# Layer 2 of a two-layer network: other places for the gate projections, the copies of the sums and the gates in a hand-written schedule

## The chip, the cores and the metric

The kernel runs on one core of one Trainium2 chip. The metric is the device time of one launch in microseconds, as the median of several runs. A profile of one further run gives each instruction's start and duration.

## The reference, cut to what matters

The program has two residual layers on an image of shape (4, 192, 128, 128). The first layer (Fourier transforms and convolutions) isn't touched by the change. The second is a selective state-space layer, with 128 x 128 = 16384 tokens per image:

```python
seq = (seq - mu) * lax.rsqrt(var + LN_EPS) * ln_g + ln_b
xz = jnp.einsum('blc,ec->ble', seq, in_proj_w)
xs, z = jnp.split(xz, 2, axis=-1)
...
u = jax.nn.silu(xc).transpose(0, 2, 1)
x_dbl = jnp.einsum('bld,kd->blk', u, x_proj_w)
dt, Bm, Cm = jnp.split(x_dbl, [DT_RANK, DT_RANK + D_STATE], axis=-1)
dt = jax.nn.softplus(jnp.einsum('blr,dr->bld', dt, dt_proj_w) + dt_proj_b)
A = -jnp.exp(A_log)
def step(hcar, inp):
    dt_t, B_t, C_t, u_t = inp
    dA = jnp.exp(dt_t[..., None] * A)
    hnew = hcar * dA + (dt_t * u_t)[..., None] * B_t[:, None, :]
    y_t = jnp.sum(hnew * C_t[:, None, :], axis=-1)
    return (hnew, y_t)
...
y = ys.transpose(1, 0, 2) + u * Dp
y = y * jax.nn.silu(z)
out = jnp.einsum('bld,cd->blc', y, out_proj_w)
```

There are 384 inner channels and 16 states. xc is a causal convolution of xs with four taps, and x comes in normalised by groups of channels. The scan over tokens is the heart of it: a decay dA, an input (dt times u times B), and a sum over states of h times C.

## The kernel before

The tokens are cut into chunks of T = 512, 32 per image, 128 in all. The 384 inner channels are three tiles of 128 partitions (j = 0, 1, 2). The 16 states are taken two at a time, so a chunk has 3 x 8 = 24 groups, k = 0 to 23; sg = k mod 8 counts within a tile. All four images run through one long list of groups (`order`), and the order of every instruction on every engine is written out by hand: nothing is scheduled automatically (`tc.manual_schedule()`).

What a group needs on the engines:

- **ACT** (ScalarE) makes the decays `da`, exp(dt A), in `decay` (L788). For most groups `early` writes them to on-chip memory four states ahead. For the groups whose inputs POOL makes (`BY_POOL`: sg 1, 4, 7, in the last tile 1 and 7), `decay_there` writes them to a PSUM buffer (`op` in the profile) three scans ahead, after the scan that frees it.
- **DVE** (VectorE) runs two scans (L856), one for each state, and for most groups the inputs' products (L808). For groups in `BY_POOL`, **POOL** (GpSimd) makes the inputs `db` (L816). For the group sg = 6 (`BY_PE`), PE turns dtu (`turned`, L822), ACT scales the four blocks for each of two states (`scaled`, L831, eight operations), and PE turns them back (`turned_back`, L842). `skip` (L896) then scales u by Dp. `TURNED` says in which group this is done for each tile.
- **POOL** multiplies h by C (`hc`, L869), and makes dtu (L745).
- **PE** (TensorE) adds the two states' hc into `py`, turned, three groups later (`sums`, L882; `LAG` = 3). There is one such PSUM buffer. After a tile's eight groups ACT copies it out (`evacuate`, L891), PE turns it back (`turn`, L911), and DVE multiplies it by silu(z) (`gate`, L916). The next tile's first sums wait for the copy. `add_skip` (L901) adds the scaled u right after those first sums, in the group sg = 3.

`front(i)` makes a chunk's inputs: the normalised x (L606), the mean's matmuls (L614) and the subtraction (L616), squares (L621), variance (L629), root (L635), reciprocal (L637), its turn (L640), copy (L643) and spread (L647), the scaling (L651), the in-projections (L657), the convolution as four matmuls a tile in two halves (L675), silu for u and z (L683, L687), the x projection (L724), its copy (L727), the store of B and C for the broadcast loads (L729, L762), the dt projections (L737), softplus (L741), and the transposes for bT (L751, L754). It is a generator that goes on by one `yield` per group. It starts at k = 14 of a chunk, for the chunk two ahead. A plain yield goes on before the group's scans; `yield MID` goes on after the group's first scan, `yield LATE` after the second. `finish` (the output projection, L925, adding to x, L931, and the store, L934) runs the same way from group 6 of the next chunk. Projections, turns and convolutions share three PSUM buffers (`psum()`).

The loop over groups around the change:

```python
                def between():
                    if done:
                        evacuate(*before)
                    go_on(parts[MID])
                    if pos >= NG and sg == LAG + 2:
                        gate(*before)

                scans(pos, n, k, between)
                go_on(parts[LATE])
```

`between` is called after the first of the group's two scans.

Of the kernel before, what the change touches and what calls it, by code (L numbers as in the profile page):

```python
# [10 lines left out]
F32 = mybir.dt.float32  # L11
# [16 lines left out]
NJ = DI // 128  # L28
NS = 16
RANK = 12  # L30
T = 512
# [472 lines left out]
def layer1(tc, xmid, out, st2, w, n_tok=S * S):  # L504
# [7 lines left out]

    BY_POOL = ((1, 4, 7), (1, 4, 7), (1, 7))
    BY_PE = 6
    TURNED = {1: 0, 10: 1, 16: 2}
    MID, LATE = "mid", "late"
    with ExitStack() as ctx:
        def pool(name, bufs, **kw):
# [64 lines left out]
        def psum():  # L583
            return ps1.tile([128, 512], F32, name="ps")
# [14 lines left out]
        def front(i):  # L599

            b, ch = divmod(i, NCHUNK)
            g = got[i]
            xm = g["xm"]
            s = lp.tile([CH, 2, T], F32, name="s", bufs=2)
            for t in range(2):
                nc.scalar.activation(  # L606
                    s[:, t, :], xm[:, t, :], AF.Identity,
                    bias=nmr[:, b, t : t + 1], scale=st2[:, b, t, 1:2],
                )
            yield  # L610
            yield
            mu = psum()
            for t in range(2):
                nc.tensor.matmul(mu[0:CH], ones[0:CH, :], s[:, t, :], start=t == 0, stop=t == 1)  # L614
            yield LATE
            nc.vector.scalar_tensor_tensor(  # L616
                s, _bc(mu[0:CH], 1, 2), -1.0 / C, s, ALU.mult, ALU.add
            )
            yield
            sq = lp.tile([128, NJ, T + 3], F32, name="xs")[0:CH, 0:2, 0:T]  # L620
            nc.scalar.activation(sq, s, AF.Square)  # L621
            yield
            yield


            var = psum()
            for q in range(4):
                for t in range(2):
                    nc.tensor.matmul(  # L629
                        var[:, q : q + 1], sq[:, t, q * 128 : (q + 1) * 128], ones[0:CH, 0:1],  # L630
                        start=t == 0, stop=t == 1,
                    )
            yield
            rs = tp.tile([128, 4], F32, name="rs")
            nc.scalar.activation(rs, var[:, 0:4], AF.Sqrt, bias=eps, scale=1.0 / C)  # L635
            yield LATE
            nc.vector.reciprocal(rs, rs)  # L637
            yield
            rt = psum()
            nc.tensor.transpose(rt[0:4, 0:128], rs, ident)  # L640
            yield MID
            rows = tp.tile([4, 128], F32, name="rows")
            nc.scalar.copy(rows, rt[0:4, 0:128])  # L643
            yield
            rb = psum()
            for q in range(4):
                nc.tensor.matmul(  # L647
                    rb[0:CH, q * 128 : (q + 1) * 128], sel[:, q, :], rows, start=True, stop=True
                )
            yield LATE  # L650
            nc.vector.tensor_tensor(s, s, _bc(rb[0:CH], 1, 2), ALU.mult)  # L651
            yield

            def in_proj(m):
                pp = psum()
                for t in range(2):
                    nc.tensor.matmul(  # L657
                        pp, wiT[:, t, m * 128 : (m + 1) * 128], s[:, t, :], start=t == 0, stop=t == 1
                    )
                return pp  # L660

            xs = lp.tile([128, NJ, T + 3], F32, name="xs")
            if ch == 0:
                nc.gpsimd.memset(xs[:, :, 0:3], 0.0)
            else:
                nc.scalar.copy(xs[:, :, 0:3], halo)
            for j in range(NJ):
                pp = in_proj(j)
                yield
                nc.scalar.activation(xs[:, j, 3:], pp, AF.Identity, bias=bxz[:, j : j + 1])  # L670
            nc.scalar.copy(halo, xs[:, :, T : T + 3])

            def conv(j, pc, half):
                for k in (2 * half, 2 * half + 1):
                    nc.tensor.matmul(  # L675
                        pc, dcw[:, j, k, :], xs[:, j, k : k + T], start=k == 0, stop=k == 3
                    )

            u, zs = g["u"], g["zs"] = {}, {}

            def silu_u(j, pc):
                u[j] = jp.tile([128, T], F32, name="u")
                nc.scalar.activation(u[j], pc, AF.Silu, bias=cb[:, j : j + 1])  # L683

            def silu_z(j, pp):
                zs[j] = jp.tile([128, T], F32, name="zs", bufs=5)
                nc.scalar.activation(zs[j], pp, AF.Silu, bias=bxz[:, NJ + j : NJ + j + 1])  # L687

            c0 = psum()
            conv(0, c0, 0)  # L690
            yield
            conv(0, c0, 1)
            yield
            c1 = psum()
            conv(1, c1, 0)
            yield
            yield
            yield
            conv(1, c1, 1)
            yield  # L700
            yield
            silu_u(0, c0)
            silu_u(1, c1)
            yield LATE
            c2 = psum()
            conv(2, c2, 0)
            yield
            conv(2, c2, 1)
            yield
            z0 = in_proj(NJ)  # L710
            yield
            yield
            silu_u(2, c2)
            silu_z(0, z0)
            yield LATE
            z1 = in_proj(NJ + 1)
            yield
            z2 = in_proj(NJ + 2)
            yield
            silu_z(1, z1)  # L720
            silu_z(2, z2)
            px = psum()
            for j in range(NJ):
                nc.tensor.matmul(px, xpT[:, j, :], u[j], start=j == 0, stop=j == NJ - 1)  # L724
            yield
            xd = tp.tile([128, T], F32, name="xd", bufs=1)
            nc.scalar.copy(xd, px)  # L727
            dbc = g["dbc"] = dram.tile([2, NS, T], F32, name="dbc")
            nc.sync.dma_start(out=dbc.rearrange("a s t -> (a s) t"), in_=xd[96:, :])  # L729
            yield  # L730
            dt, dtu = g["dt"], g["dtu"] = {}, {}


            d = [psum() for _ in range(NJ)]
            for j in range(NJ):
                rows = slice(32 * j, 32 * j + RANK)
                nc.tensor.matmul(d[j], dtT[rows, :], xd[rows, :], start=True, stop=True)  # L737
            yield
            for j in range(NJ):
                dt[j] = jp.tile([128, T], F32, name="dt")  # L740
                nc.scalar.activation(dt[j], d[j], AF.Softplus, bias=dtb[:, j : j + 1])  # L741
            yield
            for j in range(NJ):
                dtu[j] = jp.tile([128, T], F32, name="dtu")
                nc.gpsimd.tensor_tensor(dtu[j], dt[j], u[j], ALU.mult)  # L745
            yield

            bt = psum()
            for blk in range(T // 128):
                at = slice(blk * 128, (blk + 1) * 128)  # L750
                nc.tensor.transpose(bt[:, at], xd[:, at], ident)  # L751
            yield LATE
            g["bT"] = tp.tile([128, T // 128, G], F32, name="bT")
            nc.scalar.copy(  # L754
                g["bT"],
                bt.rearrange("p (k c) -> p k c", c=128)[:, :, 96 + BY_PE * G : 96 + (BY_PE + 1) * G],
            )

        def load_bc(i, sg):

# [157 lines left out]
        def finish(n):  # L918
# [3 lines left out]
            for t in range(2):  # L922
# [6 lines left out]
                yield  # L929
                yield MID  # L930
                nc.vector.tensor_add(xm[:, t, :], po[0:CH], xm[:, t, :])  # L931
                if t == 0:
                    yield
            nc.sync.dma_start(  # L934
                out=out[b][:, ch * T : (ch + 1) * T].rearrange("(t p) f -> p t f", p=CH), in_=xm
            )
# [18 lines left out]
        def go_on(fs):  # L955
            for f in fs:
                next(f, None)

        with tc.manual_schedule():
# [21 lines left out]
            for pos, (n, k) in enumerate(order):  # L981
# [1 line left out]
                if k == FRONT:  # L983
                    start_front(n + 2)
                if k == NGR - 2 and n + 1 < total:
                    assert len(fronts) == (n + 2 < total), fronts
                parts = {MID: [], LATE: []}
                step(tails, parts)

                done = pos >= NG and sg == LAG  # L990
                before = n - (j == 0), (j - 1) % NJ
                if sg == BY_PE - 1:
                    turned_back(G * (pos + 1))
                if pos >= LAG and sg != LAG:
# [10 lines left out]
                    inputs(*order[pos + 2])  # L1005

                def between():
                    if done:
                        evacuate(*before)
                    go_on(parts[MID])  # L1010
                    if pos >= NG and sg == LAG + 2:
                        gate(*before)

                scans(pos, n, k, between)
                go_on(parts[LATE])
                if k in TURNED:
                    scaled(n, TURNED[k], 0)
# [2 lines left out]
                if pos >= LAG and sg == LAG:  # L1020
                    sums(*order[pos - LAG])
                    add_skip(n, j)
                if k == LAG + 2 and n:
                    tails.append(finish(n - 1))
                if k == LAG + 7 and n + 2 < total:
                    load_x(n + 2)
                if k >= NGR - BCL and n + 1 < total:
                    load_bc(n + 1, k - (NGR - BCL))
# [148 lines left out]
```

## Time and profile before

| | |
|---|---|
| median of 3 runs | 12280.62 us (12278.13 to 12304.0) |
| profiled execution | 12415.77 us, span 12414.0 us |
| DVE busy | 10827.1 us, 87% of the span |
| PE busy | 10437.2 us, 84% |
| POOL busy | 10088.6 us, 81% |
| ACT busy | 9075.5 us, 73% |
| mean granted TensorE clock | 0.871 |

The busy shares are over both layers. The first layer takes the first eighth of the span, and DVE and POOL are less busy there. In the second layer each chunk repeats the same instructions, so windows of one chunk (some 85 us) and the timeline within it tell more than the shares. In the timelines a row has the start, the time, the engine, line and operation, and in brackets how long the engine sat idle before it and on whom it waited. Neighbouring DVE operations overlap a little, so starts are further guides than durations.

### The profile page before, as it was taken

The page shows a single profiled execution, that of the slowest core. Times are in us where ns is not written, and L with a number is a line of the kernel's source. Part 1 is how long each engine was busy: PE and PEld are TensorE (multiplying, and loading weights), DVE is VectorE, ACT ScalarE, POOL GpSimd, SP SyncE. Part 2 cuts the span into 40 slices and gives each one's busy share as a digit, 9 for nine tenths or more (in the row PEclk, how much of TensorE's full clock was granted, in tenths as well). Part 3 has the DMA queues.
Part 4 walks back from the last instruction along what each step waited for, and adds up shares of the span by engine and source line. Part 5 has one row for each costly group of instructions (what it writes and reads, how often), then busy time and mean ns, then how long its engine had stood idle before and what let it go on. Part 6 is the DMA issues. An engine that isn't in the chain of part 4 may idle for free.

```text
span 12414.0 us, 146878 instructions
## 1 busy us (share of the span) xinstructions
PE 10437.2 (84%) x49034; PEld 7035.5 (57%) x49034; DVE 10827.1 (87%) x11581; ACT 9075.5 (73%) x17891; POOL 10088.6 (81%) x4598
## 2 busy tenths in 40 slices
PE   4778888888888888888888888888888888888887
PEld 2434465555555656555555555565555555555565
DVE  5565499999999999999999899999999999999998
ACT  2322287787887877877878878778888878878777
POOL 0000199999999999999999899999999999999998
PEclk8878688888888888888888888888999888998888
DMA  8787533333323323323333233233233233233232
GB/s 212 208 215 193 165 108 102 117 106 107 117 101 112 117 94 116 113 99 117 106 107 117 99 113 117 95 115 114 98 119 119 99 113 118 99 113 117 97 114 90
DMA packets 503760, 1490.32 MB, mean 120 GB/s; under 512 B 67889, under 2 KB 118774, under 8 KB 502486
## 3 DMA queue, kind: packets, MB, share of 16 engines
q1 hardware_dynamic: 482518, 1418.00, 35.6%
q0 software_dynamic: 13312, 50.34, 1.2%
q10 hardware_dynamic: 7168, 12.59, 0.3%
q8 instruction: 385, 6.31, 0.2%
q14 instruction: 377, 3.09, 0.1%
HBM read 1325.19 MB, written 155.32 MB: 119 GB/s over the span
## 4 chain that ended last, share of the span: by engine, by line
ACT 34%; DVE 28%; PE 18%; issue 15%; POOL 3%; DMA 2%; SPq 0%; DVEq 0%; POOLq 0%; ACTq 0%
DVE h L856 18%; PE py L882 7%; ACT da L788 6%; DVE op L808 6%; ACT dbT L831 6%; ACT L788 5%; ACT op L788 4%; PE ps L675 2%; POOL hc L869 2%; PE py L901 2%; ACT u L896 2%; PE pr L471 2%; ACT dt L741 1%; ACT s L606 1%; ACT zs L687 1%
## 5 line engine op out<-in xcount | busy, mean ns | idle before, releaser
L869 POOL TENSOR_TENSOR hc<-h,bc 128x1024 f32<-128x1024 f32 x3072 | 7196.1, 2362 | 900.9 <-DVE h L856 874.8
L856 DVE TENSOR_TENSOR_SCAN h<-da,carry,op 128x512 f32<-128x512 f32 x3968 | 4896.7, 1262 | 0.3 <-DVE rs L637 0.3
L882 PE MATMUL py<-ident,hc 128*128 128x128 f32 x24576 | 3709.6, 303 | 987.1 <-ACT yt L891 574.4
L882 PEld LDWEIGHTS py<-ident,hc 128*128 128x128 f32 x24576 | 3252.7, 158 | 2085.9 <-issue 1876.2
L788 ACT ACTIVATE da<-dt,c_A_log 128x512 f32<-128x512 f32 x4096 | 2788.1, 715 | 89.6 <-DVE h L856 83.1
L856 DVE TENSOR_TENSOR_SCAN h<-op,carry,db 128x512 f32<-128x512 f32 x1984 | 2513.3, 1267 | 137.8 <-ACT op L788 135.8
L816 POOL TENSOR_TENSOR db<-dtu,bc 128x1024 f32<-128x1024 f32 x1024 | 2417.9, 2361 | 5.7 <-DMA bc<-dbc 5.7
L788 ACT ACTIVATE op<-dt,c_A_log 128x512 f32<-128x512 f32 x2048 | 1404.0, 686 | 1310.0 <-DVE h L856 1308.4
L808 DVE TENSOR_TENSOR op<-dp,bc 128x512 f32<-128x512 f32 x3328 | 2229.1, 670 | 35.9 <-DMA bc<-dbc 35.9
L675 PE MATMUL ps<-xs,dcw 128*128 128x512 f32 x3072 | 1486.2, 613 | 206.1 <-ACT u L683 206.1
L657 PE MATMUL ps<-s,c_wiT 96*128 96x512 f32 x3072 | 1465.1, 599 | 84.0 <-DVE s L651 84.0
L788 ACT ACT_TABLE_LOAD x636 | 816.0, 1283 | 214.4 <-DVE h L856 205.3
L675 PEld LDWEIGHTS ps<-xs,dcw 128*128 128x128 f32 x3072 | 562.4, 201 | 698.4 <-issue 462.0
L657 PEld LDWEIGHTS ps<-s,c_wiT 96*128 96x128 f32 x3072 | 533.9, 190 | 551.6 <-issue 407.3
L831 ACT ACTIVATE dbT<-ps,bT 128x128 f32<-128x128 f32 x3072 | 831.4, 376 | 0.0
L867 ACT COPY carry<-h 128x2 f32<-128x2 f32 x3072 | 550.1, 185 | 380.3 <-DVE h L856 374.9
L916 DVE TENSOR_TENSOR yg<-ps,zs 128x512 f32<-128x512 f32 x384 | 265.2, 691 | 534.4 <-PE ps L911 534.4
L925 PE MATMUL ps<-yg,c_woT 128*96 128x512 f32 x1536 | 700.7, 592 | 0.0
L477 POOL DMA_DIRECT2D xmid<-xt x64 | 42.6, 666 | 786.4 <-DVE xt L475 780.2
L737 PE MATMUL ps<-xd,c_dtT 12*128 12x512 f32 x768 | 457.0, 786 | 264.6 <-ACT dbT L831 263.3
L745 POOL TENSOR_TENSOR dtu<-dt,u 128x512 f32<-128x512 f32 x384 | 477.4, 1271 | 33.5 <-ACT dt L741 33.5
L842 PE MATMUL op<-ident,dbT 128*128 128x128 f32 x3072 | 463.9, 274 | 1.2 <-DVE h L856 1.2
(173 smaller groups left out, 11187.2 us busy)
## 6 DMA issues: line engine op xcount, KB each, us to landing
bc<-dbc SPq DMA_DIRECT2D x1024, 1024.0 KB, 5.4
xt<-in_x SPq DMA_DIRECT2D x192, 768.0 KB, 8.9
xmid<-xt POOLq DMA_DIRECT2D x64, 768.0 KB, 7.1
xm<-xmid SPq DMA_DIRECT2D x128, 384.0 KB, 3.5
out<-xm SPq DMA_DIRECT2D x128, 384.0 KB, 3.0
d<-x ACTq DMA_DIRECT2D x64, 192.0 KB, 6.9
df<-u SPq DMA_DIRECT2D x16, 512.0 KB, 5.0
u<-df SPq DMA_DIRECT2D x16, 512.0 KB, 12.3
```

What stands on the lines that cost most here:

```text
L657: nc.tensor.matmul(pp, wiT[:, t, m * 128 : (m + 1) * 128], s[:, t, :], start=t == 0, stop=t == 1)
L675: nc.tensor.matmul(pc, dcw[:, j, k, :], xs[:, j, k : k + T], start=k == 0, stop=k == 3)
L745: nc.gpsimd.tensor_tensor(dtu[j], dt[j], u[j], ALU.mult)
L788: nc.scalar.activation(da, got[n]["dt"][j], AF.Exp, scale=A[:, j, st : st + 1])
L808: nc.vector.tensor_tensor(dbs[s], g["dp"], g["bc", k % NG][:, 0, q, :], ALU.mult)
L816: nc.gpsimd.tensor_tensor(db, _bc(g["dtu"][j], 1, G), g["bc", sg][:, 0], ALU.mult)
L831: nc.scalar.activation(t[:, blk, :], g["tu", j][:, blk, :], AF.Identity, scale=g["bT"][:, blk, q : q + 1])
L856: nc.vector.tensor_tensor_scan(h[:, q, :], das.pop(s), dbs.pop(s) if db is None else db[:, q, :], 0.0 if ch == 0 else g["before"][:, j, st ...
L867: nc.scalar.copy(g["carry"][:, j, sg * G : (sg + 1) * G], h[:, :, T - 1])
L869: nc.gpsimd.tensor_tensor(hc, h, g["bc", sg][:, 1], ALU.mult)
L882: nc.tensor.matmul(py[:, blk, :], hc[:, q, blk * 128 : (blk + 1) * 128], ident, start=first, stop=sg == NG - 1 and q == G - 1 and blk == T ...
L925: nc.tensor.matmul(po[0:CH], woT[:, j, t * CH : (t + 1) * CH], g["yg", j], start=j == 0, stop=j == NJ - 1,)
```

## The change

In the changed kernel:

- `TURNED` is {2: 0, 10: 1, 14: 2} where it was {1: 0, 10: 1, 16: 2}.
- The copy of the sums comes after the second scan of the group sg = 2, ahead of `scaled`; it came after the first scan of sg = 3.
- The gate comes before the first scan of the group sg = 6; it came after the first scan of sg = 5.
- In `front`, the mean's matmuls come a group sooner, and the subtraction after the first scan of its group instead of the second. The root and the reciprocal come a group sooner; the scaling by the root comes in the group after, between its scans. The in-projections of xs, their copies and the first convolution come a group later.
- The first z projection comes two groups later and its silu one. The second and third z projections go from groups 13 and 14 to groups 21 and 23, and their silu from group 15 to group 0 of the next chunk. zs has four buffers, not five. So the front of one chunk is still running when two others' work begins, and the assertion counts one more.
- The dt projections are issued after the second scan of group 17 instead of before the first, and softplus after the first scan of group 18.
- The additions to x, the output's store and the next load of x come a group later.

```diff
-    TURNED = {1: 0, 10: 1, 16: 2}
+    TURNED = {2: 0, 10: 1, 14: 2}
...
             yield
-            yield
             mu = psum()
...
-            yield LATE
+            yield
+            yield MID
             nc.vector.scalar_tensor_tensor(
...
             nc.scalar.activation(sq, s, AF.Square)
             yield
-            yield
+            yield LATE
             var = psum()
...
             yield
+            yield MID
             rs = tp.tile([128, 4], F32, name="rs")
...
             yield
+            yield LATE
             rb = psum()
...
-            yield LATE
+            yield
+            yield MID
             nc.vector.tensor_tensor(s, s, _bc(rb[0:CH], 1, 2), ALU.mult)
...
-                zs[j] = jp.tile([128, T], F32, name="zs", bufs=5)
+                zs[j] = jp.tile([128, T], F32, name="zs")
...
             conv(1, c1, 0)
             yield
             yield
-            yield
             conv(1, c1, 1)
...
             conv(2, c2, 0)
             yield
+            yield
             conv(2, c2, 1)
             yield
+            yield
             z0 = in_proj(NJ)
             yield
-            yield
             silu_u(2, c2)
             silu_z(0, z0)
-            yield LATE
-            z1 = in_proj(NJ + 1)
-            yield
-            z2 = in_proj(NJ + 2)
-            yield
-            silu_z(1, z1)
-            silu_z(2, z2)
+            yield
             px = psum()
...
             nc.sync.dma_start(out=dbc.rearrange("a s t -> (a s) t"), in_=xd[96:, :])
             yield
+            yield LATE
             dt, dtu = g["dt"], g["dtu"] = {}, {}
...
                 nc.tensor.matmul(d[j], dtT[rows, :], xd[rows, :], start=True, stop=True)
             yield
+            yield MID
...
                 bt.rearrange("p (k c) -> p k c", c=128)[:, :, 96 + BY_PE * G : 96 + (BY_PE + 1) * G],
             )
+            yield
+            z1 = in_proj(NJ + 1)
+            yield
+            yield
+            z2 = in_proj(NJ + 2)
+            yield
+            silu_z(1, z1)
+            silu_z(2, z2)
...
                 nc.vector.tensor_add(xm[:, t, :], po[0:CH], xm[:, t, :])
-                if t == 0:
-                    yield
+                yield
...
-                done = pos >= NG and sg == LAG
                 before = n - (j == 0), (j - 1) % NJ
+                if pos >= NG and sg == LAG + 3:
+                    gate(*before)
...
                 def between():
-                    if done:
-                        evacuate(*before)
                     go_on(parts[MID])
-                    if pos >= NG and sg == LAG + 2:
-                        gate(*before)
 
                 scans(pos, n, k, between)
+                if pos >= NG and sg == LAG - 1:
+                    evacuate(*before)
                 go_on(parts[LATE])
...
-                if k == LAG + 2 and n:
+                if k == LAG + 3 and n:
                     tails.append(finish(n - 1))
-                if k == LAG + 7 and n + 2 < total:
+                if k == LAG + 8 and n + 2 < total:
                     load_x(n + 2)
```

More of the change, by code (lines that the diff above doesn't have):

```diff
@@ L985, in layer1 @@
                 if k == NGR - 2 and n + 1 < total:
-                    assert len(fronts) == (n + 2 < total), fronts
+                    assert len(fronts) == 1 + (n + 2 < total), fronts
                 parts = {MID: [], LATE: []}
                 step(tails, parts)
-                done = pos >= NG and sg == LAG
                 before = n - (j == 0), (j - 1) % NJ
+                if pos >= NG and sg == LAG + 3:
+                    gate(*before)
                 if sg == BY_PE - 1:
```

## The prediction

> **What bounds the kernel now.** I read the time by slices first: from 1.5 ms on every slice looks alike, so the second layer is 128 equal chunks, and one chunk is worth reading closely. Successive starts of the reciprocal (L637) in the trace are mostly 85.33 us apart, with stretches at 83.4 to 83.8; the mean of 126 steps is 84.97. A window of one chunk gives the engines' shares:
>
> ```profile
> core 0: us, PE busy (x) PEld busy (x) DVE busy (x) ACT busy (x) POOL busy (x), PEclk, DMA share, GB/s
> 5018.69:5104.02 85.33, 73.23 (x358) 50.61 (x357) 78.00 (x83) 68.14 (x137) 78.05 (x36) 0.88 0.31 108
> ```
>
> DVE and POOL each have 78 us of work and idle 7.3. The waits of the whole run say which idles first:
>
> ```profile
> POOL hc L869 <- DVE h L856: 874.8, 607, 12.0
> DVE yg L916 <- PE ps L911: 534.4, 369, 6.8
> DVE s L616 <- PE ps L614: 234.1, 128, 2.8
> DVE h L856 <- ACT op L788: 143.6, 351, 2.7
> ```
>
> POOL waits for the scans, DVE for others, so DVE's waits set the chunk. DVE's timeline shows them (bracket: idle before the row):
>
> ```profile
> 5038.04 0.69 DVE L916 TENSOR_TENSOR yg<-ps,zs 128x512 f32<-128x512 f32 x1 [2.77 <-PE ps L911]
> 5060.75 1.28 DVE L856 TENSOR_TENSOR_SCAN h<-op,carry,db 128x512 f32<-128x512 f32 x1 [0.22 <-ACT op L788]
> 5064.18 0.69 DVE L916 TENSOR_TENSOR yg<-ps,zs 128x512 f32<-128x512 f32 x1 [0.37 <-PE ps L911]
> 5068.60 1.28 DVE L856 TENSOR_TENSOR_SCAN h<-op,carry,db 128x512 f32<-128x512 f32 x1 [0.20 <-ACT op L788]
> 5071.27 1.28 DVE L856 TENSOR_TENSOR_SCAN h<-op,carry,db 128x512 f32<-128x512 f32 x1 [0.79 <-ACT op L788]
> 5077.21 1.22 DVE L616 SCALAR_TENSOR_TENSOR s<-ps,s 96x1024 f32<-96x1024 f32 x1 [1.71 <-PE ps L614]
> 5095.23 0.69 DVE L916 TENSOR_TENSOR yg<-ps,zs 128x512 f32<-128x512 f32 x1 [1.20 <-PE ps L911]
> ```
>
> They sum to 7.26 us; each also loses the 0.09 by which neighbours otherwise overlap, so 7.9 of 85.33. The largest comes by way of PE. Its timeline, and then windows of that stretch (PE and clock matter in them):
>
> ```profile
> 5030.98 1.94 PE L882 MATMUL py<-ident,hc 128*128 128x128 f32 x8 [3.79 <-ACT yt L891]
> ```
>
> ```profile
> 5027.20:5031.00 3.80, 0.01 (x1) 0.05 (x1) 3.80 (x5) 3.77 (x9) 3.80 (x2) 0.77 0.01 2
> 5031.00:5034.00 3.00, 3.00 (x15) 3.00 (x15) 3.00 (x4) 1.35 (x4) 2.92 (x3) 0.50 0.00 0
> ```
>
> PE idles 3.79 us until ACT has copied the sums out, and then runs at clock 0.50: the eight sums take 1.74 us from start to start instead of 0.87, and the turn that the gate waits for comes late.
>
> **What the Trainium skill says.** "TensorE: Matmul & The Clock Gate", Part 1: the clock halves after an idle window of about 3.4 us, and such windows run freely; the trace agrees (0.50 above), and 85.33 is 25 times 3.413. The same page, "Architectural detail", says that ACT and DVE are strict FIFO: a late ACT step delays all behind it. "ScalarE: Activation LUTs", "What ACT_TABLE_LOAD costs", gives about 1283 ns a load and a drain besides; the trace has 1283 ns, x636; a load starts 0.01 to 0.02 us after the end of the operation before it, and the page's drain of some 1380 ns doesn't appear, so I count 1.29 us a load.
>
> **The change part by part.** Group k of a chunk has scans k.a and k.b; lateness below is against the time at which DVE would come to a scan with no wait since the scan named. From DVE's timeline, start to start: scan 1.18, product 0.59, gate 0.60; two scans with products 3.54, without 2.36. From ACT's: decay 0.62, set of 8 scalings 2.01, skip 0.61, copy of sums 0.48, table load 1.29. An ACT step starts 1.30 after the start of the scan it waits for.
>
> *Gained.* The gates move one scan (1.18) on, the copies half a group sooner, the mean's matmuls a group sooner and its subtraction half a group. Waits of 2.77, 0.37, 1.20 and 1.71 go, with overlap 6.4 us. The third dt matmul no longer waits for the last scalings (PE 263.3 us in the run), but stands in PE's queue where it stood; I count it as nothing, as the next thing that DVE needs of PE lies over 5 us off.
>
> *Moved onto ACT's queue ahead of decays that DVE needs.* A decay for a POOL group goes to PSUM three scans ahead, once a scan has freed the buffer. Each chain below runs from the scan that ACT last waits for through ACT's queue to the decay. For the second scans of groups 1, 4 and 12 DVE comes there 1.77+2.36+1.77 = 5.90 after that scan.
> - 1.b: from 23.b: 1.30, decay 0.62, carry 0.20, load 1.29, two z silus 1.27, halo 0.16, load 1.29, decay 0.72: 6.85, late by 0.95. These silus stood in group 15.
> - 4.b: from 2.b: 1.30, two decays 1.24, carry 0.08, sums 0.48, scalings 2.01, skip 0.61, xs and halo 0.88, decay 0.70: 7.30, late by 1.40. The scalings stood a group earlier.
> - 12.b: the same without xs: 6.44, late by 0.54 (0.31 before).
> - 15.b: from 13.b: 1.30, decays 1.24, carry 0.20, load 1.29, silus 1.19, the two normalisings (L606) 1.52, load 1.31, decay 0.72: 8.77; due after 1.18+0.60+2.36+1.77 = 5.91, late by 2.86. Before, these silus ran in group 13, and 15.a and 15.b were late by 1.17.
> - the reciprocal, a group sooner: from 17.b: 1.30, carry 0.20, load 1.29, three softplus 1.86, load 1.29, two decays 1.24, carry 0.08, sums 0.59, load 1.29, root 0.30: 9.44; due after 5x1.77 = 8.85, late by 0.59.
>
> Sum 6.34 against 7.9: the chunk would be 83.8.
>
> *Moved onto PE.* The half convolution (1.72) now stands between the sums of group 5 and the second transposes back that scan 6.b needs. From the start of group 0, with 1.b and 4.b late: copy of sums ends at 11.8, PE adds eight sums (0.87) and waits for the skip, which follows the scalings now and ends at 14.5. From there 0.44 add, 0.87 sums, 1.72, two transposes 0.87, 0.87 sums, 1.72, 0.44: 21.5, with latency 21.7; 6.b is due at 21.8. It fits at full clock only. PE idles 1.4 and 1.8 us around those 0.87 us. In the trace a 3.413 us window busy for under 0.4 of its length was followed by half clock every time, over 0.5 hardly ever (but for the windows that hold the 12-row dt matmuls), and a half-clock window that wasn't busy nearly throughout was followed by another. Here windows that start over some 3.2 of the 3.4 us possible are below 0.5. One window at half clock costs 1.7, so 6.b is late by 1.5 (bounds: 0, no such window; 2.9, two of them). 83.8+1.5 = 85.3.
>
> *At nothing.* The centring product (L651) goes into group 23, and the matmuls that it needs are done 1 us before. xm additions, output and next load go one group on: SP's queue has output (3.0 us to landing) then load (3.5), from group 10 to group 14, some 12 us. The dbc write and the bc reads on SP keep their order, POOL's queue is unchanged. zs has four buffers for five; its silus come later, so none waits. In-projections a group later are hidden by group 3.
>
> *Sum.* 25 windows are 85.33, and 85.3 is what I get; drifting phases with an occasional 83.8 bring some 85.2. Against the profile's mean 84.97 that is +0.23, times 127: +29 us on its span of 12414. The timed runs are 134 us shorter (12278 to 12304); the trace can't say whether the first layer or the chunks were slower in the profile. I put the difference on their median: 12310. Were their chunks nearer 83.9 (all of the 134 us in them), it would be 12440.
>
> **The rivals.**
> *A (0.50): waits change places*, ACT for PE, 84.9 to 85.5 a chunk: 12270 to 12350. For it: the chains are fixed by queue order and durations from the trace. Against: 15.b alone is 2.9 of the 6.3 us, so an error there moves the whole.
> *B (0.30): faster.* PE's clock does not fall in group 3, because both idle pieces are under 1.9 us and split by sums. The place is PE before the second transposes of group 5; the price of a fall is 1.5 us a chunk, and it decides from 0.2 us of delay. Then the chunk is 83.6 to 83.8, -1.3x127 = -165: 12115, up to 12250 with falls in some chunks. For it: before, a gap of 2.85 us in group 11 left the clock at 1.00. Against: the window arithmetic.
> *C (0.18): slower by more*: two half-clock windows (86.6), or timed chunks that ran at 83.9 before: 12360 to 12480.
> *D (0.02): POOL bounds*: ACT's waits vanish, chunk 78.3, 11430. Against: the chain to 15.b.
> That the change does not do what its name says is part of A: the dt projections come no sooner in PE's queue.
>
> **How the numbers follow.** A's time is 12310. Its own range is 12250 to 12360. Over all, 12130 to 12430 leaves out half of D and B's lowest and C's upper end. A measurement here tells 0.2% (25 us) from no change. Faster: B, D and 0.03 of A, 0.35. Same: 0.15, of A. Slower: the rest of A and C, 0.50.
>
> **What would show it.** Right: no wait left before L923 (gate) and L616; DVE h <- ACT op at about 5.7 us a chunk with 2.8 of it in one place, at 15.b, the group after the one in which L690's silu stands beside L606; rs <- ACT 0.6; a DVE wait for PE before the scan after the first gate. Wrong: chunk steps under 84.5, clock 1.00 in groups 3 to 5, or ACT's wait under 3 us a chunk.

## Result and the profile after

| | before | after |
|---|---|---|
| median beside each other | 12287.46 us (12278.13 to 12304.0, 4 runs) | 12427.83 us (12376.5 to 12441.55, 4 runs) |
| ratio | 1 | 1.0105, 95% interval 1.0074 to 1.0136 |
| profiled execution, span | 12414.0 us | 12426.1 us |
| PE, DVE, ACT, POOL busy | 84, 87, 73, 81% | 82, 87, 74, 81% |
| mean granted TensorE clock | 0.871 | 0.887 |

The changed kernel is slower, by 1.05% here. The two spans differ by only 12 us: the profiled run of before took 12415.77 us, 112 to 138 more than its timed runs, and the experiments show why.

The waits of DVE in the whole run of after (microseconds in total, times, longest) answer to those shown of before:

```profile
DVE h L863 <- ACT op L795: 692.2, 509, 2.9
DVE h L863 <- PE op L849: 183.1, 247, 1.6
...
DVE rs L638 <- ACT rs L636: 78.3, 128, 5.1
...
DVE s L616 <- PE ps L613: 9.8, 2, 7.7
```

The gate, 534.4 us in before, is gone from the head of the list, and the mean's subtraction (L616) has fallen from 234.1 us in 128 waits to 9.8 in 2. ACT's decays have risen from 143.6 to 692.2 us. The waits have changed place. One chunk on DVE's timeline shows where:

```profile
5007.95 1.28 DVE L863 TENSOR_TENSOR_SCAN h<-op,carry,db 128x512 f32<-128x512 f32 x1 [0.83 <-ACT op L795]
5018.83 1.28 DVE L863 TENSOR_TENSOR_SCAN h<-op,carry,db 128x512 f32<-128x512 f32 x1 [1.34 <-ACT op L795]
5025.99 1.28 DVE L863 TENSOR_TENSOR_SCAN h<-da,carry,op 128x512 f32<-128x512 f32 x1 [1.17 <-PE op L849]
5046.06 1.28 DVE L863 TENSOR_TENSOR_SCAN h<-op,carry,db 128x512 f32<-128x512 f32 x1 [0.52 <-ACT op L795]
5057.75 1.28 DVE L863 TENSOR_TENSOR_SCAN h<-op,carry,db 128x512 f32<-128x512 f32 x1 [2.76 <-ACT op L795]
5074.25 0.18 DVE L638 RECIPROCAL rs<-rs 128x4 f32<-128x4 f32 x1 [0.53 <-ACT rs L636]
5082.39 1.28 DVE L863 TENSOR_TENSOR_SCAN h<-da,carry,op 128x512 f32<-128x512 f32 x1 [0.31 <-PE op L849]
```

In order these are scans 1.b, 4.b, 6.b, 12.b and 15.b, the reciprocal, and scan 22.b. They sum to 7.46 us, where the chunk of before had 7.26. The wait for PE at 6.b is made on PE's timeline:

```profile
5014.85 1.07 PE L889 MATMUL py<-ident,hc 128*128 128x128 f32 x8 [1.25 <-ACT yt L898]
5017.44 1.12 PE L908 MATMUL py<-ident,u 128*128 128x128 f32 x4 [1.52 <-ACT u L903]
5018.35 1.91 PE L889 MATMUL py<-ident,hc 128*128 128x128 f32 x8
5020.06 1.99 PE L678 MATMUL ps<-xs,dcw 128*128 128x512 f32 x4
...
5023.63 1.88 PE L678 MATMUL ps<-xs,dcw 128*128 128x512 f32 x4
5025.35 0.60 PE L849 MATMUL op<-ident,dbT 128*128 128x128 f32 x4
```

The idle time before the first sums has gone from 3.79 to 1.25 us, but a second one of 1.52 follows, for the skip. The windows of that stretch (length; busy time and count of PE, PEld, DVE, ACT, POOL; clock) show what it does:

```profile
5013.50:5016.85 3.35, 1.17 (x9) 0.86 (x8) 3.35 (x4) 3.35 (x13) 3.35 (x3) 1.00 0.02 5
5016.85:5020.27 3.42, 2.83 (x13) 2.83 (x14) 2.08 (x4) 3.38 (x8) 1.85 (x1) 0.50 0.00 0
```

PE was busy for 1.17 of 3.35 us, and the next window ran at clock 0.50. In it eight sums took 1.91 us, where the eight at 5014.85 took 1.07. The half convolution of 5023.63 stands right before the transposes (5025.35) that scan 6.b at 5025.99 needs.

Chunk steps, from one start of the reciprocal to the next (the first, a partial one, left out), average 85.13 us in after; 114 of the 126 are 85.33, which is 25 windows of the clock. I call such a step locked. In the profile of before they averaged 84.97.

### The profile page after: what moved, and what is told of

It is laid out like the page before. It is cut to its first block, busy times and chain, and to the rows that moved or that the text cites. A ratio compares the mean times of both kernels' runs of the same rounds, so it can differ in the third digit from the quotient of the medians.

```text
span 12426.1 us, 147265 instructions
## 1 busy us (share of the span) xinstructions
PE 10140.2 (82%) x49034; PEld 6837.2 (55%) x49034; DVE 10814.3 (87%) x11581; ACT 9163.8 (74%) x17892; POOL 10108.7 (81%) x4598
## 4 chain that ended last, share of the span: by engine, by line
DVE 30%; ACT 27%; PE 23%; issue 17%; DMA 2%; POOL 0%; SPq 0%; DVEq 0%; ACTq 0%; POOLq 0%
DVE h L863 19%; PE py L889 7%; DVE op L815 7%; ACT dbT L838 4%; ACT op L795 4%; PE ps L678 4%; ACT da L795 4%; ACT L795 3%; PE py L908 2%; PE ps L660 2%; PE op L849 2%; PE pr L471 2%; ACT dt L740 2%; ACT zs L690 2%; ACT yt L898 1%
## 5 line engine op out<-in xcount | busy, mean ns | idle before, releaser
L876 POOL TENSOR_TENSOR hc<-h,bc 128x1024 f32<-128x1024 f32 x3072 | 7208.0, 2357 | 907.8 <-DVE h L863 710.7
L863 DVE TENSOR_TENSOR_SCAN h<-da,carry,op 128x512 f32<-128x512 f32 x3968 | 4949.5, 1266 | 177.2 <-PE op L849 177.0
L889 PE MATMUL py<-ident,hc 128*128 128x128 f32 x24576 | 3573.5, 295 | 457.7 <-ACT yt L898 433.4
L889 PEld LDWEIGHTS py<-ident,hc 128*128 128x128 f32 x24576 | 3101.5, 152 | 1335.2 <-issue 854.6
L795 ACT ACTIVATE da<-dt,c_A_log 128x512 f32<-128x512 f32 x4096 | 2819.2, 718 | 433.1 <-DVE h L863 428.3
L795 ACT ACTIVATE op<-dt,c_A_log 128x512 f32<-128x512 f32 x2048 | 1428.9, 698 | 951.7 <-DVE h L863 826.3
L629 PE MATMUL ps<-ones,xs 96*128 96x1 f32 x2048 | 457.5, 354 | 366.4 <-ACT dt L740 361.6
L908 PE MATMUL py<-ident,u 128*128 128x128 f32 x1536 | 361.4, 380 | 388.1 <-ACT u L903 388.1
L629 PEld LDWEIGHTS ps<-ones,xs 96*128 96x128 f32 x2048 | 446.6, 331 | 419.5 <-ACT dt L740 411.4
L908 PEld LDWEIGHTS py<-ident,u 128*128 128x128 f32 x1536 | 255.6, 195 | 449.1 <-ACT u L903 449.1
```

The lines of the kernel that those rows point to most:

```text
L629: nc.tensor.matmul(var[:, q : q + 1], sq[:, t, q * 128 : (q + 1) * 128], ones[0:CH, 0:1], start=t == 0, stop=t == 1,)
L795: nc.scalar.activation(da, got[n]["dt"][j], AF.Exp, scale=A[:, j, st : st + 1])
L863: nc.vector.tensor_tensor_scan(h[:, q, :], das.pop(s), dbs.pop(s) if db is None else db[:, q, :], 0.0 if ch == 0 else g["before"][:, j, st ...
L876: nc.gpsimd.tensor_tensor(hc, h, g["bc", sg][:, 1], ALU.mult)
L889: nc.tensor.matmul(py[:, blk, :], hc[:, q, blk * 128 : (blk + 1) * 128], ident, start=first, stop=sg == NG - 1 and q == G - 1 and blk == T ...
L908: nc.tensor.matmul(got[n]["py", j][:, blk, :], got[n]["u"][j][:, blk * 128 : (blk + 1) * 128], ident, start=False, stop=False, is_transpos ...
```

## The experiments

Each kernel was timed beside the kernel before, so each ratio is to before on the same chip. Where a run is set against after, its median stands against 12427.83; after's nine runs on two occasions lay between 12376 and 12442. That is not a comparison side by side, and a_warm2, a_warm3, mix and the three changed forms of before were timed on other chips than a_again; there the chunk's time in the profile is the firmer figure. The table counts, from the clock's records, the half-clock windows per chunk that start in the groups named, in the profile of each kernel. The last column varies little, and nothing below rests on it.

| kernel | median us | ratio to before (95%) | chunk us | half clock in groups 3-4 | 12-13 | 16-20 |
|---|---|---|---|---|---|---|
| before | 12287.46 | 1 | 84.97 | 1.73 | 0.14 | 3.9 |
| b_again (before) | 12321.95 | 0.998 (0.9929 to 1.0031) | 84.21 | 1.00 | 0.42 | 3.6 |
| after | 12427.83 | 1.0105 (1.0074 to 1.0136) | 85.13 | 0.98 | 0 | 4.0 |
| a_again (after) | 12433.68 | 1.0092 (1.0076 to 1.0107) | 85.13 | 0.98 | 0 | 4.0 |
| a_conv_late | 12293.92 | 0.9943 (0.9902 to 0.9983) | 84.02 | 0.94 | 0.34 | 3.7 |
| a_warm2 | 12382.09 | 0.9992 (0.996 to 1.0023) | 84.70 | 0 | 0.79 | 3.6 |
| a_warm3 | 12238.33 | 0.9853 (0.9836 to 0.9869) | 83.58 | 0 | 0.60 | 3.5 |
| a_scal_early | 12126.14 | 0.9808 (0.9768 to 0.9848) | 82.65 | 0 | 0.53 | 3.5 |
| a_silu_back | 12153.71 | 0.983 (0.979 to 0.987) | 82.9 | 0.32 | 0 | 3.7 |
| b_gate | 12323.4 | 0.9948 (0.9916 to 0.998) | 84.21 | 1.69 | 0.72 | 4.0 |
| b_gate_copy | 12213.98 | 0.9858 (0.9828 to 0.9889) | 83.49 | 1.48 | 0 | 4.0 |
| b_full | 12128.95 | 0.9762 (0.9747 to 0.9776) | 82.78 | 0 | 0 | 3.5 |
| mix | 11901.03 | 0.9606 (0.9575 to 0.9636) | 80.97 | 0 | 0 | 3.8 |
| mix_nine | 11802.62 | 0.9586 (0.9573 to 0.9599) | 80.14 | 0 | 0 | 3.6 |

**Before once more** (b_again: no edit).

> The kernel before, unchanged. The changed kernel is 1.05% slower (some 130 us), while the two profiles differ by 12 us only. Theory: the kernel before has two rhythms, chunk steps of 85.33 us and of 83.4 to 83.8 us; its first profile caught mostly the first, its timed runs (12278 to 12304) mostly the second. Then an execution near 12290 shows a mean chunk step near 83.9 and the same time up to the second layer. Rival: the steps stay near 85 and the time up to the second layer is shorter by some 130 us.

Its profiled span was 12303.2 us, 111 less than the first profile of the same kernel. The steps averaged 84.21 us, and 33 of 126 were 85.33, where it had been 92. That is 96 of the 111 us; the other 15 lie ahead of the second of the layer's reciprocals, where these steps begin (at 1505.0 us for 1519.8). Half-clock windows in groups 3 and 4 went from 1.73 to 1.00 a chunk. From first scan to first scan, chunks of this profile with such a window took 85.05 us on average, those without one 82.52. So the time of before depends on how many of its chunks have the fall of the clock. Its other runs, which have no trace, fit this: over the 31 that were timed beside the experiments, from 12287.86 to 12431.5 us, the mean clock falls from 0.880 to 0.869 nearly in step. The chip alone doesn't decide it: the four runs of b_again, on one chip, took 12305.02 to 12408.84 us.

**The half convolution after the transposes** (a_conv_late):

```diff
             conv(0, c0, 1)
             yield
+            yield LATE
             c1 = psum()
             conv(1, c1, 0)
```

> The changed kernel with the first half of the second convolution after group 5's scans, so behind the second transposes back in PE's queue instead of ahead of them. Theory (PE's queue at half clock makes scan 6.b late by 1.5 us a chunk): the wait of DVE for L849 goes, chunk steps of 83.8, 190 us less than the changed kernel. Rival (the chunk is held at 25 clock windows whatever one wait is): steps stay at 85.33 and another wait grows, under 40 us of gain.

134 us less than after. The clock still falls in groups 3 and 4 (0.94 windows a chunk), but DVE's wait for PE at the scans falls from 8.8 us in a stretch of 512 to 1.4. So the fall alone doesn't make 6.b late; the half convolution in front of its transposes is needed too. The gain was smaller than the 190 forecast, in part because two waits of 1.0 us came back at the gate in that stretch.

**PE fed in group 3** (a_warm2, then a_warm3):

```diff
             conv(0, c0, 0)
-            yield
             conv(0, c0, 1)
             yield
+            yield
             c1 = psum()
             conv(1, c1, 0)
-            yield
-            yield
             conv(1, c1, 1)
+            yield
+            yield
```

> The kernel after, with the first tile's second half convolution taken from group 4 into group 3 (into PE's idle time around the sums) and the second tile's second half taken from group 7 into group 5. So between the adding of the skip and the second transposes of group 5 PE has as much work as after (two half convolutions, 3.44 us), but its idle time of 2.8 us in group 3 shrinks to some 1.2. If the fall of the clock makes scan 6.b late, no half-clock window follows group 3, DVE's wait for PE at the scans goes from 8.8 us in 512 to under 3, and the chunk is 83.7 to 84.1: some -130 us against after, about 12295. If the length of the queue does it, 6.b is as late as after or later, and the time is within 0.3% of after or above it.

The time came out 46 us under after, between the two theories. The clock stayed full in group 3, as meant, but 6.b still waited 0.78 us, because both halves now stood together behind transposes that wait for a scan; and the clock now fell in groups 12 and 13, which in the chunk read cost scan 14.b 1.85 us and shortened 15.b's wait to 0.81. The run changed two things at once. a_warm3 keeps PE's order between the skip and 6.b:

```diff
             conv(0, c0, 0)
-            yield
             conv(0, c0, 1)
             yield
             c1 = psum()
             conv(1, c1, 0)
             yield
-            yield
             conv(1, c1, 1)
```

> The kernel after, with three half convolutions one slot sooner: the first tile's second half from group 4 into group 3, the second tile's first half from group 5 into 4, its second half from 7 into 5. Between the adding of the skip and the second transposes of group 5 PE's queue holds exactly the work it holds after, two half convolutions at the same places; only its idle time in group 3 is shorter (1.3 us or so for 2.8). If the clock's fall makes scan 6.b late, no half-clock window starts in groups 3 and 4 and 6.b waits under 0.3 us (1.17 after). In the run with both halves of a tile together the fall went to groups 12 and 13 once it was gone from group 4, and cost the scan of group 14 what group 15 then gained; if that comes again the chunk is 83.8 to 84.3 all the same, some -120 us against after, 12310. If the queue's order alone makes 6.b late it waits 1.0 or more at full clock, and the time stays at 12380 or above.

The same stretch on PE's timeline, with the same work in the same order from the skip on:

```profile
5044.86 0.66 PE L908 MATMUL py<-ident,u 128*128 128x128 f32 x4 [1.26 <-ACT u L903]
5045.35 1.04 PE L889 MATMUL py<-ident,hc 128*128 128x128 f32 x8
5046.22 1.88 PE L678 MATMUL ps<-xs,dcw 128*128 128x512 f32 x4
...
5049.69 1.88 PE L678 MATMUL ps<-xs,dcw 128*128 128x512 f32 x4
5051.41 0.60 PE L849 MATMUL op<-ident,dbT 128*128 128x128 f32 x4
```

From the skip's adding to the second transposes it is 6.55 us, where after took 7.91. Scan 6.b doesn't wait, no step is 85.33 any more, and the time is 189 us below after, for 120 forecast. With a_conv_late this settles it: 6.b was late because the clock fell and the half convolution stood in front.

**The first tile's scalings in group 1 again** (a_scal_early):

```diff
-    TURNED = {2: 0, 10: 1, 14: 2}
+    TURNED = {1: 0, 10: 1, 14: 2}
```

> The changed kernel with the first tile's scalings a group sooner, in group 1 as before. Theory: the decay for 4.b is no longer behind them (1.34 + 0.09 us less a chunk), add_skip doesn't wait for the skip, PE has no 1.5 us idle there and keeps its clock, and the wait before 6.b (1.17) goes too: 2.7 us a chunk, some 340 us less. Rival: the scalings in group 1 hold up the xs copies or the decays of group 2 and half or more is given back: under 170 us.

302 us less than after, for 340 forecast. The wait at 4.b is gone, and 6.b's is 0.38; no half-clock window starts in groups 3 and 4, as the skip comes sooner, too. ACT's decays wait 24.1 us in the stretch of 512 for 32.8.

**The third convolution, first z projection and their silus in group 13 again** (a_silu_back):

```diff
             conv(2, c2, 0)
             yield
-            yield
             conv(2, c2, 1)
             yield
-            yield
             z0 = in_proj(NJ)
             yield
+            yield
             silu_u(2, c2)
             silu_z(0, z0)
             yield
+            yield
             px = psum()
```

> The changed kernel with the second half of the third convolution, the first z projection and the silus of u2 and z0 each back in the group they had before (10, 11 and 13). Theory: the wait before 15.b falls from 2.85 (with lost overlap) to some 1.6, as the table load no longer waits for scan 13.b: 1.2 us a chunk, 150 us less. Rival: with PE's queue as the true bound of the chunk the wait before 6.b grows by as much, under 40 us.

274 us less, nearly twice the forecast. The 2.76 us at 15.b became 0.69 and 0.79; the rest came by way of PE, for which DVE now waited 3.4 us in the stretch instead of 8.8, as half-clock windows in groups 3 and 4 became rare (0.32 a chunk). PE's idle pieces in group 3 had not changed; the section on the prediction comes back to this.

**Before with the gate moved, and with gate and copy moved** (b_gate has the gate's lines of the change, with the additions to x and the load; b_gate_copy the copy's also).

> The kernel before with the gate alone moved from after the first scan of group 5 of a tile to ahead of group 6 (and the additions to x and the load a group on with it). The gate comes 1.18 us of DVE work later, so its waits of 2.77, 0.37 and 1.20 should become 1.6, 0 and 0; the mean's wait of 1.71 and ACT's 1.2 stay. Chunk 77.4+4.5+overlap = 82.2, up to 83.3 where the freed time comes back as waits for ACT: -100 to -240 us against before. If instead the gain of the whole change is lost only by what the z silus and scalings add on ACT, this is already most of what there is to gain from the gates.

> The kernel before with the gate as in the run before this and the copy of the sums at the end of group 2 ahead of all else on ACT there: the parts of the change that take waits away, without those that load ACT's queue (z silus, scalings, root). PE's idle time in group 3 shrinks below 2 us or so, and no half-clock window follows. No wait at the gate; left are the mean's 1.71 and ACT's 1.2 to 1.9. Chunk 80.6 to 81.2, so some -400 us against before, 11870. Rival: the copy ahead of the decays makes scans of groups 3 and 4 late in each tile, and the chunk stays above 82.5.

Both fell short: 77 and 187 us below before as it ran beside them. In b_gate the gate still waited up to 2.08 us, and L616 2.48. In b_gate_copy the copy came sooner, and PE still sat idle in group 3 almost as long:

```profile
5040.22 1.94 PE L882 MATMUL py<-ident,hc 128*128 128x128 f32 x8 [3.16 <-ACT yt L891]
```

and ran at half clock behind it. My count of 1.25 us of idle time had come with the in-projections and the half convolution that the change moves into groups 2 and 3; without them there is nothing to run there.

**All that took waits away, with ACT's work where it was** (b_full: b_gate_copy, and the mean, the scaling by the root, the in-projections and the dt projections as after, the first half convolution of the second tile as in a_conv_late; `TURNED`, the reciprocal and all z silus stay in their groups of before).

> The kernel before with all that took a wait away and nothing that moved ACT's work ahead of a decay: gate and copy as after, the mean's matmuls and subtraction sooner, the scaling by the root and with it the in-projections and first convolution a group later (they give PE work in group 3), dt projections as after. All z silus, the scalings and the reciprocal stay in their groups of before. The gates' copy without the later in-projections left PE idle for 3.2 us in group 3 and half-clock windows behind it; with them the gap should be filled. If so, no half-clock window in groups 3 to 5, no wait at the gates and at the mean, none at 1.b; left are 0.5 at 12.b and 1.3 to 1.6 in groups 14 and 15: chunk 79.8 to 80.6, 11780 to 11860, at or below the best so far (11901). If the z silus at the chunk's end are needed to relieve groups 14 and 15, it stays above 11950.

No half-clock window in groups 3 and 4, no wait at the gate, none at 1.b: that much was right. But the time was 12129 us, some 300 above the forecast, because the mean's wait was back, on DVE's timeline

```profile
5055.20 1.22 DVE L616 SCALAR_TENSOR_TENSOR s<-ps,s 96x1024 f32<-96x1024 f32 x1 [2.30 <-PE ps L613]
```

and PE's timeline says for whom its matmuls waited:

```profile
5053.20 1.96 PE L613 MATMUL ps<-s,ones 96*96 96x512 f32 x4 [0.98 <-ACT zs L691]
```

The mean a group sooner needs one of the three buffers of `psum()`, and the z silus of group 15 still hold it. In after and in mix, where these silus run at the chunk's end, L616 doesn't wait in the stretches read. So the z projections at the chunk's end are what makes the earlier mean possible: they cost 0.83 us at 1.b and save 2.30 here. (mix differs from b_full in the third tile's scalings as well; that PE waits for L691 is what speaks for the silus.)

**After with its costs undone** (mix: a_conv_late, a_scal_early, a_silu_back, and the reciprocal after its group's two scans instead of ahead of them, which the second `yield LATE` does; mix_nine: also the second tile's scalings in group 9).

```diff
-    TURNED = {2: 0, 10: 1, 14: 2}
+    TURNED = {1: 0, 9: 1, 14: 2}
...
             nc.scalar.activation(rs, var[:, 0:4], AF.Sqrt, bias=eps, scale=1.0 / C)
             yield LATE
+            yield LATE
             nc.vector.reciprocal(rs, rs)
```

> The kernel after with four of its moves undone together: the half convolution later, the first scalings in group 1 again, the third convolution, first z projection and their silus as before in group 13, and the reciprocal at the end of its group. If the waits add up as the chains say, what is left is 0.95 at scan 1.b, 0.5 at 12.b and 1.2 to 1.6 in group 15: chunk 80.0 to 80.6, some 11800 to 11870 (-560 us or so against after). If the single gains overlap (waits that only change place) it stays above 12000.

> The best version so far with the second tile's scalings in group 9 instead of 10, as the first tile's stand in group 1 instead of 2. Moving the first tile's took the whole wait of 1.35 us at scan 4.b; this should take the 0.53 at 12.b: with the overlap 0.62 a chunk, 79 us, some 11825. POOL, which is 96% busy in the best version (78.1 us of 80.97), leaves room for it. If POOL or ACT hand the time back elsewhere, it stays within 25 us of 11901.

mix is 527 us below after, at 80.97 us a chunk a little over the forecast of 80.0 to 80.6. mix_nine takes another 98, for 79 forecast; the 0.53 at 12.b is gone. mix_nine beats both kernels, by 4.1% against before (0.9586, 0.9573 to 0.9599). DVE's waits in a stretch of 512 us of mix_nine, and the stretch itself:

```profile
DVE h L865 <- ACT op L797: 15.5, 20, 1.0
DVE h L865 <- PE op L851: 2.3, 3, 1.2
DVE h L865 <- POOL db L825: 0.4, 2, 0.2
```

```profile
5000.00:5512.00 512.00, 438.29 (x2264) 297.31 (x2262) 493.76 (x522) 437.86 (x870) 495.80 (x223) 0.92 0.33 114
```

18.2 us of waits are left, and POOL, busy for 495.80 of 512, is within 3.2% of being the bound.

**After once more** (a_again: no edit).

> The kernel after, unchanged, measured once more beside the kernel before. The kernel before took 12278 to 12304 us when the change was first measured, and 12318 to 12431 since; the kernel after took 12376 to 12442. If the 1% by which the change was slower is what the rhythm of the chunks of before happened to be in those runs, after stays at 12380 to 12440 here, and the ratio lies between 0.998 and 1.009, nearer 1.0 when before runs long. If the change costs 1% whatever the rhythm, after moves along with before and the ratio is 1.008 or more again.

After took 12396.71 to 12438.77 us, as in its first measurement, with the same 114 locked steps. The kernel before ran short here, at 12287.86 to 12368.14, so the ratio was 1.0092. Both branches of the expectation allow that, so this run doesn't decide between them. Whether after would also be level with before where that runs at 12414 to 12431 stays open: the two were never timed beside each other there.

## Why the prediction was right on the mechanism and short on the size

**Waits change places: right.** The chains of the prediction, and what the chunk above shows with the 0.09 us of lost overlap added (the means over the run are within 0.04 us of this chunk's idle times):

| place | predicted us late | measured |
|---|---|---|
| 1.b | 0.95 | 0.92 |
| 4.b | 1.40 | 1.43 |
| 12.b | 0.54 | 0.61 |
| 15.b | 2.86 | 2.85 |
| reciprocal | 0.59 | 0.62 |
| 6.b, by PE | 1.5 | 1.26 |
| 22.b, by PE | not foreseen | 0.40 |
| sum | 7.84 | 8.09 |

Each ACT chain was right because ACT runs its queue in order ("TensorE: Matmul & The Clock Gate", "Architectural detail", in the Trainium skill, says strict FIFO). ACT's timeline of group 14 shows the longest one link by link:

```profile
5051.75 1.28 ACT L686 ACT_TABLE_LOAD   x1
5053.05 0.69 ACT L686 ACTIVATE u<-ps,c_cb 128x512 f32<-128x512 f32 x1
5053.63 0.68 ACT L690 ACTIVATE zs<-ps,bxz 128x512 f32<-128x512 f32 x1
5054.20 1.51 ACT L606 ACTIVATE s<-xm,nmr,st 96x512 f32<-96x512 f32 x2
5055.73 1.28 ACT L795 ACT_TABLE_LOAD   x1
5057.02 0.69 ACT L795 ACTIVATE op<-dt,c_A_log 128x512 f32<-128x512 f32 x1
```

The last line ends at 5057.71; scan 15.b starts at 5057.75.

**The clock's fall: right for this kernel, its odds too high.** Rival B, that the two idle pieces would leave the clock alone, fell. One half-clock window a chunk starts in groups 3 and 4 (0.98). Its price was a little high: of the window's 3.42 us PE worked 2.83, which loses 1.4 us (an estimate: half of 2.83), not 1.7. The Trainium skill, same page, "Why this matters for your kernels", asks for no idle gap over about 3 us; here two gaps of 1.25 and 1.52 us with sums between them were enough, and the measurement decides. Rival C's two windows didn't come, and D's POOL stayed behind DVE (it waited for the scans, 710.7 us in the run). The wait at 22.b was not foreseen, and no run looked for its cause.

The prediction also held that windows starting over 3.2 of the 3.4 us possible would be under half busy, so that nearly any chunk would have the fall. a_silu_back says otherwise. PE sits idle for the same two pieces there, and most chunks keep their clock (0.32 windows a chunk for 0.98). In this chunk each piece lies in a window of its own, and both windows are over half busy:

```profile
5105.57 1.06 PE L889 MATMUL py<-ident,hc 128*128 128x128 f32 x8 [1.25 <-ACT yt L898]
5108.16 0.66 PE L908 MATMUL py<-ident,u 128*128 128x128 f32 x4 [1.53 <-ACT u L903]
```

```profile
5102.39:5105.81 3.42, 2.17 (x7) 0.84 (x6) 3.42 (x4) 2.43 (x7) 3.42 (x3) 1.00 0.02 6
5105.81:5109.22 3.41, 1.88 (x18) 1.64 (x17) 2.39 (x3) 3.38 (x11) 3.41 (x2) 1.00 0.00 0
```

In after, a locked chunk starts at the same point of a window every time, and for group 3 it is a bad one. A like pair of 1.19 and 1.53 us in groups 11 and 12 of after's chunk above (before 5042.90 and 5045.49) leaves the clock alone; the table has 0 there. So the fall in nearly every chunk goes with the lock; no run shifted the start of the windows alone. What a fall costs the chunk was near the forecast in a_silu_back too: from first scan to first scan, chunks with one took 83.90 us on average, those without 82.58.

**The chunk: right.** 85.2 was predicted, 85.13 measured. The profile's span was to grow by 29 us and grew by 12: the step was 0.16 us longer instead of 0.23 (20 us for 29), what lies ahead of the steps was 11 us shorter in that execution, and what lies behind them 3 longer.

**The time: 118 us short.** 12310 was forecast and 12427.83 measured, outside the 12250 to 12360 of rival A. The step that failed is "I put the difference on their median". It set a difference that was worked out against the profile's steps of 84.97 upon timed runs that had run in the shorter rhythm. b_again's profile shows that rhythm: steps of 84.21 us. From there to 85.13 is 0.92 x 126 = 116 us, and with what lies ahead of the steps and behind them after's profiled execution is 123 us above b_again's, where 29 had been added: 94 of the 118. The other 24 are that the three timed runs of before (median 12280.62) were shorter still than b_again's profiled one (12305.02); no trace of them was kept, so why is open.

The branch that the prediction named beside it, "Were their chunks nearer 83.9", gave 12440, 12 us from the result; it stood in rival C at 0.18, together with a second half-clock window that didn't come. That the result lies within the range over all, 12130 to 12430, is luck: by 2 us, and five of after's nine runs were above 12430.

**"Gained" held only as a whole.** The later gate alone gained 77 us (b_gate), with the sooner copy 187 (b_gate_copy), for lack of work for PE in group 3; the mean's wait went only with the z silus (b_full). The dt projections were costed at nothing; no run tried them alone.

**What the costs were worth.** Undone one at a time they gave 134, 302 and 274 us; undone together, with the reciprocal, 527. The single gains overlap: each of the three takes most of the same wait at 6.b away, whose mean over the run was 1.14 us in after and 0, 0.39 and 0.43 in them.

## What to carry to other kernels

Set a predicted difference only on runs that you know to be like the one it was worked out against: if a profile is 1% longer than the timed runs, find out which chunks differ before adding. When a step is moved on an in-order queue, run the chain to the next operation that has the least slack; here five such sums were right within 0.07 us. And look at what a move leaves behind as well: idle pieces on PE that fall into one clock window can take the clock down as one long gap does. Whether they do depends on where the window starts, so count them over several chunks and not in one.

## What the hardware showed that was not expected

- Chunks of before and after lock to 25 clock windows. Stretches at half clock start on a grid of 3.413 us, which held to 0.02 us over the second layer in every trace, and 25 of that are 85.33: 92 of 126 steps in one profile of before, 33 in another, 114 in both of after. In a_warm3, where no half-clock window delays 6.b, there is none. The same program thus ran at 12278 to 12431 us, and after, with nearly all steps locked, at 12376 to 12442.
- Most of the other kernels lock too, several chunks at a time. From first scan to first scan, two chunks of b_gate_copy are 167.25 us (49 windows, to within 0.08 us for 85% of the pairs), three of a_conv_late 252.58 (74 windows, 81%), four of mix 324.27 (95 windows, 83%). Half of b_again's chunks go three to 74 windows, so the shorter rhythm of before is partly a lock as well. b_full shows none up to eight chunks. What makes a kernel settle on one was not tried.
- With group 3 fed, 0.5 to 0.8 windows a chunk fell in groups 12 and 13, where none had in after. In a_warm2 and a_warm3 the idle pieces there are those of after, 1.2 and 1.5 us; what differs is where the windows start. These falls cost little, because a later ACT wait shrank by about as much: 14.b and 15.b together wait 2.71 us a chunk in a_warm3, and 2.77 in after.
